# A two-layer graph kernel: attention in pairs of key blocks, and another order of work in the last block

## The chip, the cores and the metric

The kernel runs on one core of one Trainium2 chip. The metric is device time in microseconds (us) for one launch, and the number compared is the median over runs. A profiled execution is one run with the hardware profiler on. Its span is the time from the first to the last instruction.

Engines: PE is TensorE's matmul row, PEld its weight loads, DVE VectorE, ACT ScalarE, POOL GpSimd, SP SyncE, which here issues DMAs. L436 is line 436 of the kernel before.

## The reference, cut to what matters

There are 32 samples of 512 nodes with 512 features, all in fp32, and one 512 x 512 adjacency matrix for all samples. Layer 0 is a graph layer, layer 1 masked attention with 8 heads of 64. Each has a residual and a layernorm.

```
x = layernorm(x + deg * (x @ Wi.T + b) + adj @ (x @ Wj.T))     # layer 0
q, k, v = split_heads(x @ Wq.T + bq), ...                      # layer 1
scores = einsum('bhqd,bhkd->bhqk', q, k) / 8
scores = where(adj == 0, -inf, scores)
attn   = softmax(scores)
x = layernorm(x + (attn @ v) @ Wo.T + bo)
```

## The kernel before, in words

**Products.** Every 512 x 512 by 512 x 512 product (layer 0's two, q, k, v and the output projection) is done with seven half-size products in place of eight. Each is a *piece* (`piece`, L411 on): products 1 to 7, of kind l0, v, q, k or pj (projection). A piece is four matmuls with 256 columns (eight records in the profile, as an fp32 matmul leaves two); an l0 piece has twice as many, as it takes two weights. Its sums and differences of inputs come from `combos` on POOL (L405), its weights from DRAM through a ring of seven SBUF tiles that SP fills in order (`prefetch`, L286). It writes into one of two PSUM banks, "a" and "b" (`mm_tile`, one buffer each). The products fall into groups (X: 1, 2; Y: 6, 7, 4; Z: 5, 3), and those of a group add up in the same bank, so that each piece is read out by DVE or ACT before the next piece in its bank may write. Kinds are alternated between the two banks. DVE adds l0 and pj pieces to the rows (L454), v to v (L465), q and k with their bias (L481) or without (L474); ACT copies product 1 (L443) and writes product 2 of v (L463), q and k (L479).

**Attention.** A block of work is one sample's attention: 8 steps, `divmod(step, 4)` giving a group g of four heads and a block kc of 128 keys. A step does the following:
- `scores` twice: two heads at a time, two matmuls on 64 rows each into a PSUM tile "sc" of two banks. There are two such tiles. ACT takes the exponential in place (L494), DVE multiplies by the mask into an SBUF tile "e" (L495; four such buffers).
- `values` of the step before: eight matmuls of 32 columns each into two "ov" tiles (L512).
- at the last block of keys of a group, `sums` (denominators, L522, into an sc tile), `drain` by ACT (L527), and then `rest`: four reciprocals (`invert`, L531), two `scale` (L547) and `tell` (L535) on DVE.
- `presum`: e tiles of a group are added up, the first two on POOL (L501), the others on DVE (L503).

[...]

**Order.** Engines work through their queues in the order in which the program issues instructions; nothing reorders it (`manual_schedule`). The order is written by hand. While sample b = n - 1 has its attention, the pieces of layer 0, v, q, k of sample n and the projection of sample n - 2 fill the steps. `phase_b`, `phase_c` and `phase_a` list them with entries of no cost (`z`) between: statistics (`stats`: bn_stats and bn_aggr on DVE, then L300 to L302 on POOL), `apply` on ACT (L305), the rows' way through DRAM into transposed form (`h_store` on ACT's queue, `h_load` on SP's, `h_turn` on DVE, L382), `l0_gather` (L334, adjacency by rows, copied out by ACT, followed by `split`: a cast on ACT and a subtraction on POOL, L204), `l0_turn` (L348 on DVE, L349 on POOL), `base` (L354, DVE). `by_steps` deals the list out to the eight steps by the cost PC, TR or GA of each entry. For a middle block this gives:

```
0  l0_2  combos  pj1  l0_6  pj2
1  combos  l0_7  add_bo0  pj6  l0_4  stats(n,0)  pj7
2  apply(n,0)  h_store0  l0_5  h_load0  add_bo1  pj4  l0_3  stats(n,1)  h_turn0  pj5
3  apply(n,1)  h_store1  v1  pj3  h_load1  stats(m,0)  v2  stats(m,1)  q1  k1  apply(m,0)  h_turn1  q2
4  apply(m,1)  store  combos  k2  q5  v5  q3  v3
5  load_x  q6  v6  q7  v7  q4  v4  (with load_xa, ahead)
6  gather0  k5  turn0  gather1  k3  turn1  base0  combos  gather2  k6
7  turn2  base1  gather3  k7  turn3  combos  l0_1  k4
```

Here n is the sample in layer 0 and m = n - 2; k pieces of steps 6 and 7 use the bank that gathers do not use. Behind each piece or gather the main loop issues one presum that is due, and entries of `rest`.

**The end.** The last sample's attention has only the projection of the sample before it to fill its steps (`last_steps`), its own projection (`last_part`, L735 and L736, in four row blocks) and the last rows' layernorm (`last_rows`).

Of the kernel before, what the change touches and what calls it, by code (L numbers as in the profile page):

```python
# [17 lines left out]
P = 128  # L18
# [7 lines left out]
def gnn_attention_kernel(  # L26
# [53 lines left out]
    def work(shape, name, bufs, dtype=FT):  # L80
        return pools.work.tile(shape, dtype, name=name, bufs=bufs)
# [10 lines left out]
    def sc_tile():  # L92
        return psum.tile([P, 2, N], FT, name="sc", bufs=2)
# [189 lines left out]
    def prefetch():  # L283
        while len(TILES) < min(len(KEYS), ring.used + RING) and KEYS[len(TILES)] in WS:
            t = ring_tile()
            nc.sync.dma_start(t, WS[KEYS[len(TILES)]])  # L286
            TILES.append(t)
# [193 lines left out]
                    nc.vector.scalar_tensor_tensor(d[:, c], pm[:, c, :], bc, p1[:, c, :], op0=OP.add, op1=OP.add)  # L481


    E, ES, PV, RL = {}, {}, {}, {}

    def scores(b, hp, kc):
        ps = sc_tile()
        for s in range(2):
            r = slice(s * HD, (s + 1) * HD)
            nc.tensor.matmul(ps[:, s, :], KT[b, hp // 2][r, hp % 2, kc * P:(kc + 1) * P],  # L490
                             QT[b, hp // 2][r, hp % 2, :], start=True, stop=True)
        e = E[hp % 2, kc] = work([P, 2, N], "e", 4)

        nc.scalar.activation(ps, ps, AF.Exp, scale=QSCALE)  # L494
        nc.vector.tensor_tensor(e, ps, edge[:, kc:kc + 1, :].to_broadcast([P, 2, N]), op=OP.mult)  # L495

    def presum(i, kc):
# [7 lines left out]
    def values(b, g, kc):  # L505

        if kc == 0:
            PV[g] = [ov_tile(), ov_tile()]
        for r in range(2):
            for h in range(4):  # L510
                c0 = (4 * g + h) * HD + 32 * r
                nc.tensor.matmul(PV[g][r][32 * h:32 * h + 32, :], V[b][:, kc, c0:c0 + 32], E[h // 2, kc][:, h % 2, :],  # L512
                                 start=(kc == 0), stop=(kc == NC - 1))
# [12 lines left out]
        j = 2 * (b * 2 + g)  # L526
        nc.scalar.activation(RL[g][1], RL[g][0], AF.Identity, accum_out=told[:, j:j + 1])  # L527

    def invert(g, part, src=1):
        c = slice(part * P, (part + 1) * P)  # L530
        nc.vector.reciprocal(RL[g][1][:, c], RL[g][src][:, c])  # L531

    def tell(b, g):
        j = 2 * (b * 2 + g) + 1
        nc.vector.reduce_sum(told[:, j:j + 1], RL.pop(g)[1], axis=AX.X)  # L535

    def tell_all(b, g):

        pl, rl = RL.pop(g)
        j = 2 * (b * 2 + g)  # L540
        nc.gpsimd.memset(told[:, j + 1:j + 2], 0.0)
        nc.vector.tensor_tensor_reduce(pl, pl, rl, 1.0, 0.0, OP.add, OP.add, told[:, j:j + 1])

    def scale(b, g, r, c=slice(0, N)):
        if (b, g) not in OT:
# [14 lines left out]
    def z(f, *a):  # L560
        return (0.0, f, *a)

    def pc(kind, b, i, bank):
        return (2 * PC if kind == "l0" else PC, piece, kind, b, i, bank)
# [1 line left out]
    ORDER = (1, 2, 6, 7, 4, 5, 3)  # L566

    LATE = (5, 3, 6, 7, 4)
    ALONE = ((1, "a"), (6, "b"), (2, "a"), (7, "b"), (5, "a"), (4, "b"), (3, "a"))

    def banks(n):

# [2 lines left out]
    def phase_a(n):  # L575

        A, K = banks(n)
        if n == B:
            return [pc("k", n - 1, i, bank) for i, bank in ((6, K), (5, A), (7, K), (3, A), (4, K))]
        xq, aq = lambda j, m: quarter(XD[n], j, m), lambda j, m: quarter(AX_T[n], j, m)  # L580
        g = [(GA, l0_gather, n, dc, A) for dc in range(DC)]
        k = [pc("k", n - 1, i, K) for i in LATE]
        res = []
        for i in range(DC):
            res += g[i:i + 1] + k[i:i + 1] + [z(l0_turn, n, i)]
            if i in (1, 2):
                res += [z(base, n, i - 1)]
            if i == 1:
                res += [z(combos, TX, n, xq, (1,)), z(combos, TA, n, aq, (1,))]
        return res + [z(combos, TX, n, xq, (2,)), z(combos, TA, n, aq, (2,)),  # L590
                      z(combos, TX, n, xq, (3, 4)), z(combos, TA, n, aq, (3, 4)),
                      pc("l0", n, 1, A), k[4]]
# [27 lines left out]
    def project(m, i):  # L620

        res = [pc("pj", m, i, banks(m)[1])]
        if i == 1:
            res = [z(combos, TO, m, ot_quarter(m), (1,))] + res
        if i == 2:
            res = [FLUSH] + res + [z(combos, TO, m, ot_quarter(m), (2, 3, 4))]
        return res

    def phase_b(n):

        m = n - 2
        if m < 0:
            res = []
            side = [z(add_bo, 0, i) for i in range(2)]
            A, K = banks(n)
            for i, bank in ((2, A), (6, K), (5, A), (7, K), (4, K), (3, A)):
                res.append(pc("l0", n, i, bank))
                if i == 4:
                    res += [z(stats, n, 0)]
                if i in (2, 6):  # L640
                    res += [z(combine, "wo", nc.vector, int(i == 6))]
                res += side[:1]
                side = side[1:]
            return res + [z(apply, n, 0), z(stats, n, 1), (TR, l0_norm, n, 0), (TR, l0_norm, n, 1)]
        A = banks(n)[0]
        l0 = {i: pc("l0", n, i, A) for i in ORDER}
        return [l0[2], *project(m, 1), l0[6], *project(m, 2), l0[7], z(add_bo, n - 1, 0), *project(m, 6), l0[4], z(stats, n, 0),
                *project(m, 7), z(apply, n, 0), z(h_store, n, 0), l0[5], z(h_load, n, 0), z(add_bo, n - 1, 1), *project(m, 4),
                l0[3], z(stats, n, 1), z(h_turn, n, 0), *project(m, 5)]

    def phase_c(n):

# [53 lines left out]
    def last_steps():  # L706

        m = B - 2
        p = {i: pc("pj", m, i, bank) for i, bank in ALONE}
        c = [z(combos, TO, m, ot_quarter(m), (1, 2)), z(combos, TO, m, ot_quarter(m), (3, 4))]  # L710
        own = [(4 * GA, last_part, c, 0) for c in range(2)]
        return [[z(last_load), FLUSH, c[0], p[1], c[1]], [p[2], p[6]], [p[5], p[7], z(add_bo, B - 1, 0), z(add_bo, B - 1, 1)],
                [p[3], p[4], z(stats, m, 0), z(stats, m, 1)], [z(apply, m, 0), z(apply, m, 1), z(store, m)], [own[0]], [own[1]], []]

    def run(f):
        f[1](*f[2:])
# [8 lines left out]
    def last_part(c, half=None, ic=None):  # L725
        if c == 0:
            if half == 0:
                ACC[0], ACC[1] = mm_tile("a"), mm_tile("b")
            else:
                t = sc_tile()  # L730
                ACC[2], ACC[3] = t[:, 0, :], t[:, 1, :]
        for ic in (range(2 * half, 2 * half + 2) if ic is None else (ic,)):
            if c == 0:

                nc.tensor.matmul(ACC[ic], ident, XT[B - 1][:, ic, :], start=True, stop=False)  # L735
            nc.tensor.matmul(ACC[ic], OT[B - 1, c // 2][:, c % 2, ic * P:(ic + 1) * P], W["wo"][c // 2][:, c % 2, :],  # L736
                             start=False, stop=(c == 3))
# [32 lines left out]
    for f in PERIODS[0]:  # L770
        run(f)
        if f[1] is combine:
            prefetch()
    for n in range(1, B + 1):
        b = n - 1
        extra = []
        for step in range(STEPS):
            g, kc = divmod(step, NC)
            scores(b, 2 * g, kc)
            scores(b, 2 * g + 1, kc)  # L780
            pb, pg, pk = (b, *divmod(step - 1, NC)) if step > 0 else (b - 1, 1, NC - 1)
            if pb >= 0:
                values(pb, pg, pk)
                if pk == NC - 1:
                    sums(pg, *(((1, 3), 3) if pb == B - 1 else ()))
                    drain(pb, pg)
                    extra = rest(pb, pg)
            late = [(presum, i, kc) for i in range(2) if kc > 0]
            if b == B - 1 and kc > 2 - g:

                late = []
            for f in PERIODS[n][step]:
                if f is FLUSH:
                    some = len(extra)
                else:
                    run(f)

                    some = 0 if f[0] == 0.0 else len(extra) if step == 0 else max(1, round(f[0] / PC))
                if some:
                    for g in late[:1] + extra[:some]:  # L800
                        g[0](*g[1:])
                    late, extra = late[1:], extra[some:]
            for g in late + extra:
                g[0](*g[1:])
            extra = []
    sums(1, (1, 2), 3)
    values(B - 1, 1, 3)
    sums(1, (3,), 3)
    for c in range(2):
        last_part(c, 1)  # L810
    for ic in range(NC):
        c = slice(ic * P, (ic + 1) * P)
        invert(1, ic, 0)
        scale(B - 1, 1, 0, c)
        scale(B - 1, 1, 1, c)
        last_part(2, ic=ic)
        last_part(3, ic=ic)
        if ic > 0:
            last_rows(ic - 1)
    tell_all(B - 1, 1)  # L820
    last_rows(NC - 1)
    flags()
    fast.close()
# [139 lines left out]
```

## Time and profile before

| what | value |
|---|---|
| median of 10 runs | 3694.5 us (3692.47 to 3696.34) |
| profiled execution: its time | 3693.48 us |
| its span | 3691.7 us |
| PE, PEld busy | 3661.8, 2510.9 us |
| DVE, POOL, ACT busy | 2393.1, 1940.8, 1028.5 us |
| mean granted TensorE clock | 0.999 |
| DMA queue 1's share of the 16 engines | 49.4% |
| exponentials (L494), masks (L495) | 512 each, 1007 and 1217 ns |
| presums on DVE (L503), on POOL (L501) | 250 of 1217 ns, 128 of 2360 ns |

A matmul's end in the profile is modelled and neighbours overlap, so lengths of matmul work are read from start to start. "Idle before, releaser" tells which event ended an engine's idle time. Instructions that follow one another on an engine are merged in a timeline; the number behind the x counts them. In a timeline the first column is the start in us from the span's start, the second the length in us.

### The profile page before, as it was taken

The numbers are of one execution on the slowest core, as the hardware profiler recorded it, in microseconds if no ns is written. First come the engines' busy times: TensorE is split into PE (matmuls) and PEld (weight loads), VectorE is DVE, ScalarE is ACT, GpSimd is POOL, SyncE is SP. The second block draws the span as 40 slices with busy tenths as digits, with TensorE's granted clock in tenths as the row PEclk, the third lists the DMA queues.
The fourth block names the chain that finished last, engine by engine and source line by source line (L and its number), as shares of the span: only waits on it lengthen the run. The fifth ranks groups of instructions, "written<-read, shape, count | busy, mean of one in ns | idle before, by whom it ended". The sixth has DMA issues, their size and how long they took to land.

```text
span 3691.7 us, 49640 instructions
## 1 busy us (share of the span) xinstructions
PE 3661.8 (99%) x18470; PEld 2510.9 (68%) x18470; DVE 2393.1 (65%) x3134; ACT 1028.5 (28%) x1483; POOL 1940.8 (53%) x1985
## 2 busy tenths in 40 slices
PE   9999999999999999999999999999999999999997
PEld 6766667676667666767676767676767676767663
DVE  4666666666666666666666666666666666666665
ACT  2232232222322223222223222222222322222322
POOL 3565545556445555455554555644555545555443
PEclk9999999999999999999999999999999999999999
DMA  8445455445555445564455555455544555445541
GB/s 256 140 120 143 138 155 160 136 133 137 149 159 150 130 134 147 151 166 122 138 140 152 160 146 127 133 151 157 155 125 136 144 156 162 130 134 139 149 137 47
DMA packets 797173, 530.02 MB, mean 144 GB/s; under 512 B 530432, under 2 KB 611840, under 8 KB 796928
## 3 DMA queue, kind: packets, MB, share of 16 engines
q1 hardware_dynamic: 780384, 494.78, 49.4%
q10 hardware_dynamic: 16320, 31.46, 2.3%
q8 instruction: 151, 2.47, 0.3%
q14 instruction: 94, 0.77, 0.1%
q0 software_dynamic: 224, 0.53, 0.0%
HBM read 453.25 MB, written 73.40 MB: 143 GB/s over the span
## 4 chain that ended last, share of the span: by engine, by line
PE 98%; DVE 1%; POOL 0%; ACT 0%; issue 0%; DMA 0%; SPq 0%; ACTq 0%; DVEq 0%; POOLq 0%
PE mma L436 31%; PE mmb L436 31%; PE sc L490 13%; PE ov L512 13%; PE mmb L334 4%; PE mma L334 3%; PE sc L522 2%; PE mmb L611 0%; PE mma L611 0%; DVE rl L531 0%; DVE e L495 0%; PE sc L736 0%; DVE st L298 0%; POOL es L501 0%; DMA big<-in_adj_dram 0%
## 5 line engine op out<-in xcount | busy, mean ns | idle before, releaser
L494 ACT ACTIVATE sc<-sc 128x1024 f32<-128x1024 f32 x512 | 493.0, 1007 | 1554.8 <-PE sc L490 1548.8
L495 DVE TENSOR_TENSOR e<-sc,edge 128x1024 f32<-128x1024 f32 x512 | 602.2, 1217 | 212.1 <-ACT sc L494 179.7
L436 PE MATMUL mmb<-ring,big 128*128 128x256 f32 x3144 | 731.7, 381 | 0.0
L436 PE MATMUL mma<-ring,big 128*128 128x256 f32 x3112 | 724.4, 381 | 1.5 <-DVE xh L454 0.8
L436 PEld LDWEIGHTS mmb<-ring,big 128*128 128x128 f32 x3144 | 591.9, 190 | 131.6 <-issue 27.7
L436 PEld LDWEIGHTS mma<-ring,big 128*128 128x128 f32 x3112 | 585.8, 190 | 132.4 <-issue 26.5
L490 PE MATMUL sc<-q,k 64*128 64x512 f32 x2048 | 509.0, 615 | 0.0
L405 POOL TENSOR_TENSOR big<-big 128x512 f32<-128x512 f32 x376 | 492.3, 1338 | 28.4 <-ACT big L363 12.5
L512 PE MATMUL ov<-e,v 128*32 128x512 f32 x4096 | 492.5, 598 | 4.9 <-DVE oT L547 4.9
L501 POOL TENSOR_TENSOR es<-e 128x1024 f32<-128x1024 f32 x128 | 300.6, 2360 | 355.1 <-DVE e L495 355.1
L436 PE MATMUL mma<-big,ring 128*128 128x256 f32 x1808 | 430.3, 381 | 0.0
L436 PE MATMUL mmb<-big,ring 128*128 128x256 f32 x1776 | 422.8, 381 | 1.0 <-DVE v L465 1.0
L300 POOL TENSOR_SCALAR mv<-mv 128x1 f32<-128x1 f32 x256 | 50.1, 196 | 674.0 <-DVE mv L299 661.7
L436 PEld LDWEIGHTS mma<-big,ring 128*128 128x128 f32 x1808 | 340.5, 190 | 73.1 <-issue 26.0
L436 PEld LDWEIGHTS mmb<-big,ring 128*128 128x128 f32 x1776 | 334.3, 190 | 73.5 <-issue 26.0
L512 PEld LDWEIGHTS ov<-e,v 128*32 128x32 f32 x4096 | 106.9, 109 | 352.2 <-issue 320.8
L204 POOL TENSOR_TENSOR xlo<-xh,xhi 128x512 fp32r<-128x512 f32 x128 | 162.9, 1285 | 338.8 <-ACT xhi L203 338.7
L490 PEld LDWEIGHTS sc<-q,k 64*128 64x128 f32 x2048 | 176.0, 186 | 207.4 <-issue 205.1
L349 POOL TENSOR_TENSOR big<-big,deg_r 128x512 f32<-128x512 f32 x124 | 173.5, 1399 | 263.5 <-DVE big L348 263.5
L503 DVE TENSOR_TENSOR es<-es,e 128x1024 f32<-128x1024 f32 x250 | 304.1, 1217 | 0.0
L454 DVE TENSOR_TENSOR xh<-xh,mma 128x512 f32<-128x512 f32 x186 | 126.7, 681 | 263.5 <-PE mma L436 263.5
L454 DVE TENSOR_TENSOR xh<-xh,mmb 128x512 f32<-128x512 f32 x186 | 126.7, 681 | 259.3 <-PE mmb L436 259.3
(161 smaller groups left out, 3662.4 us busy)
## 6 DMA issues: line engine op xcount, KB each, us to landing
ring<-wo SPq DMA_DIRECT2D x217, 256.0 KB, 2.8
ring<-wq SPq DMA_DIRECT2D x160, 256.0 KB, 3.9
ring<-wv SPq DMA_DIRECT2D x160, 256.0 KB, 3.4
ring<-wk SPq DMA_DIRECT2D x160, 256.0 KB, 3.2
ring<-wi SPq DMA_DIRECT2D x155, 256.0 KB, 2.6
ring<-wj SPq DMA_DIRECT2D x155, 256.0 KB, 2.6
xh<-in_x_dram SPq DMA_DIRECT2D x32, 1024.0 KB, 5.4
xa<-in_x_dram SPq DMA_DIRECT2D x124, 256.0 KB, 3.9
```

Source lines behind the costliest of these rows:

```text
L204: nc.gpsimd.tensor_sub(lo, xs, hi.bitcast(FT))
L334: nc.tensor.matmul(pm, parts[w][:, jc, :], adjR[:, jc, :], start=(w == 0 and jc == 0), stop=(w == 1 and jc == NC - 1))
L349: nc.gpsimd.tensor_tensor(XD[b][:, dc, :], XD[b][:, dc, :], deg_r, op=OP.mult)
L405: nc.gpsimd.tensor_tensor(dst, p, q, op=OP.subtract)
L436: nc.tensor.matmul(pm[:, c * Q:(c + 1) * Q], lhs, rhs, start=first, stop=(kc == 1 and n == len(terms) - 1), skip_group_check=True)
L454: nc.vector.tensor_tensor(d, d, pm, op=OP.add)
L490: nc.tensor.matmul(ps[:, s, :], KT[b, hp // 2][r, hp % 2, kc * P:(kc + 1) * P], QT[b, hp // 2][r, hp % 2, :], start=True, stop=True)
L494: nc.scalar.activation(ps, ps, AF.Exp, scale=QSCALE)
L495: nc.vector.tensor_tensor(e, ps, edge[:, kc:kc + 1, :].to_broadcast([P, 2, N]), op=OP.mult)
L501: nc.gpsimd.tensor_add(ES[i], E[i, 0], E[i, 1])
L503: nc.vector.tensor_add(ES[i], ES[i], E[i, kc])
L512: nc.tensor.matmul(PV[g][r][32 * h:32 * h + 32, :], V[b][:, kc, c0:c0 + 32], E[h // 2, kc][:, h % 2, :], start=(kc == 0), stop=(kc == NC - 1))
```

## The change

It has two parts.

**Attention in four steps of two blocks of keys.** For all samples but the last, the main loop goes two steps at a time. It issues the scores of the first block of keys, the values of both blocks that are due, the masks of the first block, and at a group's end sums, drain and rest; then the scores of the second block, and then the pieces of both steps. The mask leaves `scores` and becomes an operation of its own. The masks of the second block, `tell` and the presums (four for kc = 2, 3, two for kc = 0, 1) are issued one by one behind pieces; at a group's end the reciprocals and scales are issued before the pieces, otherwise the first of these masks is. In the list, `apply(n,0)` and `h_store0` come ahead of pj7, `h_load0` ahead of l0_5, `h_turn0` ahead of l0_3; nothing is issued between l0_3 and `stats(n,1)`.

**The end.** Of the last sample's five remaining k pieces, 7 and 4 move into its first attention step; the projection before it takes the usual order of pieces, with 3 and 4 one step each behind; statistics, apply and store of that sample move behind it. The final denominators are drained by ACT and inverted in SBUF; the last two row blocks get an sc tile each and their first two parts are issued between those of the first two.

```diff
     def scores(b, hp, kc):
...
+        SC[hp] = ps
+
+        nc.scalar.activation(ps, ps, AF.Exp, scale=QSCALE)
+
+    def mask(hp, kc):
+        ps = SC.pop(hp)
         e = E[hp % 2, kc] = work([P, 2, N], "e", 4)
-
-        nc.scalar.activation(ps, ps, AF.Exp, scale=QSCALE)
         nc.vector.tensor_tensor(e, ps, edge[:, kc:kc + 1, :].to_broadcast([P, 2, N]), op=OP.mult)
...
-        return [l0[2], *project(m, 1), l0[6], *project(m, 2), l0[7], z(add_bo, n - 1, 0), *project(m, 6), l0[4], z(stats, n, 0),
-                *project(m, 7), z(apply, n, 0), z(h_store, n, 0), l0[5], z(h_load, n, 0), z(add_bo, n - 1, 1), *project(m, 4),
-                l0[3], z(stats, n, 1), z(h_turn, n, 0), *project(m, 5)]
+                z(apply, n, 0), z(h_store, n, 0), *project(m, 7), z(h_load, n, 0), l0[5], z(add_bo, n - 1, 1), *project(m, 4),
+                z(h_turn, n, 0), l0[3], z(stats, n, 1), *project(m, 5)]
...
+        k = [pc("k", B - 1, i, K) for i in (7, 4)]
+        return [[z(last_load), k[0], FLUSH, c[0], p[1], c[1], k[1]], [p[2], p[6]], [p[5], p[7], z(add_bo, B - 1, 0), z(add_bo, B - 1, 1)],
+                [p[3]], [p[4]], [own[0], z(stats, m, 0), z(stats, m, 1)], [own[1], z(apply, m, 0), z(apply, m, 1), z(store, m)], []]
...
+        alone = b == B - 1
+        size = 1 if alone else 2
+        for step in range(0, STEPS, size):
             g, kc = divmod(step, NC)
+            extra = []
+            for i in range(2):
+                scores(b, 2 * g + i, kc)
+            for f in due:
+                values(*f)
+            for i in range(2):
+                mask(2 * g + i, kc)
+            if due and due[-1][2] == NC - 1:
+                pb, pg = due[-1][:2]
+                sums(pg, *(((1, 3), 3) if pb == B - 1 else ()))
+                drain(pb, pg)
+                extra = rest(pb, pg)
+            due = [(b, g, kc + i) for i in range(size)]
+            late = [(presum, i, c) for _, _, c in due if c > 0 for i in range(2)]
+            if alone:
...
+            else:
+                for i in range(2):
+                    scores(b, 2 * g + i, kc + 1)
+                late = [(mask, 2 * g + i, kc + 1) for i in range(2)] + extra[-1:] + late
+
+                for f in extra[:-1] if extra else late[:1]:
+                    f[0](*f[1:])
+                late, extra = late[0 if extra else 1:], []
+            for f in [f for todo in PERIODS[n][step:step + size] for f in todo]:
...
+                    if f[1] is piece and f[2] == "l0" and f[4] == 3:
+
+                        some = 0
                 if some:
                     for g in late[:1] + extra[:some]:
                         g[0](*g[1:])
...
     sums(1, (3,), 3)
-    for c in range(2):
-        last_part(c, 1)
+    drain(B - 1, 1)
     for ic in range(NC):
         c = slice(ic * P, (ic + 1) * P)
-        invert(1, ic, 0)
+        invert(1, ic)
         scale(B - 1, 1, 0, c)
         scale(B - 1, 1, 1, c)
+        if ic < 2:
+            last_part(0, 1, ic + 2)
+            last_part(1, 1, ic + 2)
         last_part(2, ic=ic)
         last_part(3, ic=ic)
```

More of the change, by code (lines that the diff above doesn't have):

```diff
@@ L481, in piece @@
                     nc.vector.scalar_tensor_tensor(d[:, c], pm[:, c, :], bc, p1[:, c, :], op0=OP.add, op1=OP.add)
-    E, ES, PV, RL = {}, {}, {}, {}
+    SC, E, ES, PV, RL = {}, {}, {}, {}, {}
     def scores(b, hp, kc):
@@ L527, in drain, with invert @@
         nc.scalar.activation(RL[g][1], RL[g][0], AF.Identity, accum_out=told[:, j:j + 1])
-    def invert(g, part, src=1):
+    def invert(g, part):
         c = slice(part * P, (part + 1) * P)
-        nc.vector.reciprocal(RL[g][1][:, c], RL[g][src][:, c])
+        nc.vector.reciprocal(RL[g][1][:, c], RL[g][1][:, c])
     def tell(b, g):
@@ L535, in tell @@
         nc.vector.reduce_sum(told[:, j:j + 1], RL.pop(g)[1], axis=AX.X)
[L537 to L542, printed above, removed]
     def scale(b, g, r, c=slice(0, N)):
@@ L568, in gnn_attention_kernel @@
     LATE = (5, 3, 6, 7, 4)
-    ALONE = ((1, "a"), (6, "b"), (2, "a"), (7, "b"), (5, "a"), (4, "b"), (3, "a"))
     def banks(n):
@@ L578, in phase_a @@
         if n == B:
-            return [pc("k", n - 1, i, bank) for i, bank in ((6, K), (5, A), (7, K), (3, A), (4, K))]
+            return [pc("k", n - 1, i, bank) for i, bank in ((5, A), (6, K), (3, A))]
         xq, aq = lambda j, m: quarter(XD[n], j, m), lambda j, m: quarter(AX_T[n], j, m)
@@ L708, in last_steps @@
         m = B - 2
-        p = {i: pc("pj", m, i, bank) for i, bank in ALONE}
+        A, K = banks(B)
+        p = {i: pc("pj", m, i, K if i in (6, 7, 4) else A) for i in ORDER}
         c = [z(combos, TO, m, ot_quarter(m), (1, 2)), z(combos, TO, m, ot_quarter(m), (3, 4))]
         own = [(4 * GA, last_part, c, 0) for c in range(2)]
-        return [[z(last_load), FLUSH, c[0], p[1], c[1]], [p[2], p[6]], [p[5], p[7], z(add_bo, B - 1, 0), z(add_bo, B - 1, 1)],
-                [p[3], p[4], z(stats, m, 0), z(stats, m, 1)], [z(apply, m, 0), z(apply, m, 1), z(store, m)], [own[0]], [own[1]], []]
+        k = [pc("k", B - 1, i, K) for i in (7, 4)]
+        return [[z(last_load), k[0], FLUSH, c[0], p[1], c[1], k[1]], [p[2], p[6]], [p[5], p[7], z(add_bo, B - 1, 0), z(add_bo, B - 1, 1)],
+                [p[3]], [p[4]], [own[0], z(stats, m, 0), z(stats, m, 1)], [own[1], z(apply, m, 0), z(apply, m, 1), z(store, m)], []]
     def run(f):
@@ L729, in last_part @@
             else:
-                t = sc_tile()
-                ACC[2], ACC[3] = t[:, 0, :], t[:, 1, :]
+                ACC[ic] = sc_tile()[:, 0, :]
         for ic in (range(2 * half, 2 * half + 2) if ic is None else (ic,)):
@@ L773, in gnn_attention_kernel @@
             prefetch()
+    due = []
     for n in range(1, B + 1):
         b = n - 1
-        extra = []
-        for step in range(STEPS):
+        alone = b == B - 1
+        size = 1 if alone else 2
+        for step in range(0, STEPS, size):
             g, kc = divmod(step, NC)
[L779 to L792, printed above, removed]
+            extra = []
[13 more added lines that the diff above has]
+            if alone:
+                if kc > 2 - g:
+                    late = []
+            else:
[6 more added lines that the diff above has]
+            for f in [f for todo in PERIODS[n][step:step + size] for f in todo]:
                 if f is FLUSH:
@@ L795, in gnn_attention_kernel @@
                 else:
+                    if f[1] is l0_norm:
+                        for g in late:
+                            g[0](*g[1:])
+                        late = []
                     run(f)
-                    some = 0 if f[0] == 0.0 else len(extra) if step == 0 else max(1, round(f[0] / PC))
+                    some = 0 if f[0] == 0.0 else len(extra) if step == 0 and alone else max(1, round(f[0] / PC))
+                    if f[1] is piece and f[2] == "l0" and f[4] == 3:
+                        some = 0
                 if some:
@@ L804, in gnn_attention_kernel @@
                 g[0](*g[1:])
-            extra = []
     sums(1, (1, 2), 3)
@@ L819, in gnn_attention_kernel @@
             last_rows(ic - 1)
-    tell_all(B - 1, 1)
+    tell(B - 1, 1)
     last_rows(NC - 1)
```

## The prediction

> **What bounds the kernel now.** I read the busy shares and the chain first, then the matmuls of one block in order of time, then the whole trace for holes in TensorE's row, then one stretch with VectorE and GpSimd beside it.
>
> ```profile
> PE 3661.8 (99%) x18470; PEld 2510.9 (68%) x18470; DVE 2393.1 (65%) x3134; ACT 1028.5 (28%) x1483; POOL 1940.8 (53%) x1985
> ...
> PE 98%; DVE 1%; POOL 0%; ACT 0%; issue 0%; DMA 0%; SPq 0%; ACTq 0%; DVEq 0%; POOLq 0%
> ```
>
> TensorE sets the time. So only two things count: the time that its own instructions take, and new holes between them. The timeline of TensorE over one step (start, us, what) shows what a change of shape costs:
>
> ```profile
> 1841.55 1.99 PE L490 MATMUL sc<-q,k 64*128 64x512 f32 x8
> 1843.47 1.93 PE L512 MATMUL ov<-e,v 128*32 128x512 f32 x16
> 1845.33 1.99 PE L436 MATMUL mma<-ring,big 128*128 128x256 f32 x8
> 1847.16 1.89 PE L436 MATMUL mmb<-ring,oT 128*128 128x256 f32 x8
> 1848.88 1.89 PE L436 MATMUL mma<-ring,big 128*128 128x256 f32 x8
> ...
> 1859.54 1.04 PE L522 MATMUL sc<-es,ones 128*32 128x512 f32 x8
> ```
>
> A piece takes 1.73 us from start to start, but 1.83 when it comes first after values. From the starts of the single matmuls (steady spacing 216 ns in pieces, 429 ns in scores, values and sums) the changes cost: into scores 93 + 104 = 197 ns, into values 97 + 25 = 122 ns, into pieces 113 + 104 = 217 ns, from values into sums nothing. Between 160 and 3570 us no other hole over 0.3 us exists. The steady kernel has no stall to remove, only these changes.
>
> The last block differs, and shows how a hole arises:
>
> ```profile
> 3588.03 1.89 PE L436 MATMUL mmb<-ring,big 128*128 128x256 f32 x8
> 3590.90 1.99 PE L436 MATMUL mmb<-big,ring 128*128 128x256 f32 x8 [0.98 <-DVE v L465]
> ...
> 3646.80 1.93 PE L512 MATMUL ov<-e,v 128*32 128x512 f32 x16 [3.09 <-DVE oT L547]
> ```
>
> A piece waits until VectorE has read the piece before it out of the same bank. VectorE was late because two presums (1.2 us each) stood in its queue.
>
> The stretch of steps 6 and 7 is the one to watch (TensorE, VectorE and GpSimd of one timeline):
>
> ```profile
> 1892.97 1.89 PE L436 MATMUL mma<-big,ring 128*128 128x256 f32 x8
> ...
> 1896.54 1.89 PE L436 MATMUL mma<-big,ring 128*128 128x256 f32 x8
> ...
> 1896.60 3.42 DVE L354 SCALAR_TENSOR_TENSOR xh<-b_r,deg_c,xh 128x512 f32<-128x512 f32 x2 [0.21 <-POOL xlo L204]
> ...
> 1897.88 3.28 POOL L405 TENSOR_TENSOR big<-big 128x512 f32<-128x512 f32 x2
> 1898.36 1.99 PE L490 MATMUL sc<-q,k 64*128 64x512 f32 x8
> 1899.94 0.68 DVE L474 TENSOR_TENSOR k<-mma,k 128x512 f32<-128x512 f32 x1
> ...
> 1904.09 1.89 PE L436 MATMUL mma<-big,ring 128*128 128x256 f32 x8
> ```
>
> k6 ends at about 1898.3 and is read out only at 1899.94, behind base (3.42 us). Nobody waits: scores and values of step 7 fill 3.8 us, and k7 starts at 1904.09.
>
> [...] 122 to 217 ns per change, and none from values to sums, which are tiled alike. [...] 124 of 128 base operations lie on a GpSimd one and the median is 1.75 us, against 0.71 for those that meet it late or not; presums beside add_bo took 1.76 and 1.70 us instead of 1.21.
>
> **The change, part by part.** I call the new pairs 0-1, 2-3, 4-5 and 6-7, and count t from a pair's first scores.
>
> *Fewer changes of shape.* Two old steps have scores, values and pieces twice: 2 x (197 + 122 + 217) = 1072 ns. A pair has scores, values (both blocks), scores, pieces. Values to scores is not in the steady trace; one sums-to-scores change shows the 113 ns of its class, so I take 97 + 104 = 201 (bounds 0[...], and 217). New sum 197 + 122 + 201 + 217 = 737. Gain 0.335 us per pair (0.32 to 0.54), 31 blocks x 4 pairs: **-41.5 us** (-40 to -67).
>
> *Do the second scores wait for their tiles?* First masks need the e buffers that the first values release, at t = 1.92 + 1.93 + 0.06 = 3.9. Two masks take 2.35, so the second tile is free at 6.3. TensorE ends both values at 5.49 and needs the first tile (free 5.1) at 5.6, the second at 6.55. Where sums lie between, sums take the first tile, scores need the second at 6.46. Slack 0.15 to 0.25 us: nothing lost while VectorE and ScalarE are on time. Pieces start at 7.5 (8.4 with sums). In 2-3 they are not quite on time: apply and h_store of half 0 now stand in ScalarE's queue ahead of the exponentials, and wait for the statistics (GpSimd needs 1.2 us for each block of rows), so that the exponentials start at 3.3 to 3.6 instead of 1.2: 0.1 to 0.5 us, I take 0.3.
>
> *6-7: the pause is gone, four presums stand before k6's read-out.* TensorE: gather0 7.5-9.55, k5 to 11.3, gather1 13.1, k3 14.85, gather2 16.7, k6 18.4, gather3 20.26, then k7. VectorE in order: k5 read-out from 11.45 (0.80), presum 1.13, turn 0.62, presum 1.13 (now 15.13), k3 0.80 (15.93), presum 1.13, turn 0.62 (17.7), base 3.35 (21.05), presum 1.13 (22.2), k6 0.69: 22.9. k7 waits 22.9 - 20.26 = 2.7 us. Before, two of these presums came after k7's start. If base met no GpSimd work (2 x 0.71) it would be 0.7; if, as the order of the queues suggests, GpSimd's turn product and xlo also catch the third and fourth presum, these add up to 2.0: 4.7. I take 3.6. 30 blocks have gathers: **+108 us** (20 to 141).
>
> *2-3: v2 waits for v1's copy.* l0[3] ends at 16.2; VectorE reads it out to 17.0, statistics to 18.7, GpSimd's chain ends 20.4 to 20.6 (before: 4.4 us after l0[3]), apply to 21.3, the h_store issue up to 0.37, only then ScalarE copies v1 (0.6): 21.9 to 22.4. v2 could start at 21.4. Before, scores and values (3.8 us) lay between. 0.5 to 1.0, I take 0.7; with the 0.3 above 1.0 x 30 = **+30 us** (18 to 45).
>
> *4-5: reciprocals and scales in one run.* Sums end 6.35, drain ends 7.3, four reciprocals 3.4, two scales 1.3: 12.0. Then a mask (13.2), q5's read-out (14.0). q3 could start at 13.65: 0.4 x 30 = **+12 us** (0 to 20). In 0-1 the first piece is an l0 one of 3.5 us and ends at 11.9, so VectorE is back in time: nothing. If that cover were a short piece, the same 0.4 would appear there.
>
> *Moves with no path cost.* h_load 0 passes l0[5] on SP: it waits for h_store, about 3.4 us, with ring prefetches behind it, covered by seven ring tiles (12 us of pieces); uncovered it would cost up to 3.4 us a block. h_turn 0 ahead of l0[3]: 1.25 us of VectorE, which is idle then. h_turn 1 is late in 4-5 only if its load comes after t = 3.9; I get 2.6, as apply is earlier by the 1.9 us of exponentials. Presums on GpSimd end before the masks that reuse their inputs (26.6 against 32).
>
> *The end.* The last 135 us hold some 9.7 us of holes, of 0.4 to 3.1 us. Two k pieces now fill the step after the first denominators (about -1.4) and statistics no longer precede the masks (-2.0). p4 in step 4 delays the reciprocals by its own 1.9 + 0.65, so that hole stays. The final denominators go through ScalarE (+0.7), the row blocks' own tiles free VectorE from the 1.5 us wait on ScalarE. Sum **-4** (-8 to +2). The first pair of block 0 has no values to cover its masks: **+2** (0 to 3).
>
> Against the profiled execution's 3693.5 us (span 3691.7 and 1.8 around it): 3693.5 - 41.5 + 108 + 30 + 12 - 4 + 2 = 3800.0. The median of the runs is 1.0 higher: **3801 us**, +2.9%.
>
> **Rivals.** *Forecast, bank waits outweigh the changes saved:* for it, VectorE's queue in 6-7 counted instruction by instruction and the 3590.90 line; against it, the size hangs on how GpSimd's operations fall. Range 3735 to 3850. Chance 0.66.
> *Faster, the bank waits don't hold TensorE:* one mechanism: read-outs keep ahead of the same bank's next piece, as they do throughout the steady trace. It decides where the waits of a block sum to less than 4 x 0.335 = 1.34 us. Then 3693.5 - 41.5 - 4 + 2 + 30 x 0.3 = 3659, median 3660. For it: nothing waits today. Against it: the 3.8 us pause that hid the late read-out is what is removed. 0.17.
> *Same:* base and presums meet no GpSimd work: 0.7 in 6-7, 0.5 in 2-3, none in 4-5: -43.5 + 36 = 3686 to 3700. 0.05.
> *Slower elsewhere, the score tiles:* if VectorE begins the first masks late by one mask (1.2 us), the second scores lose about 0.95 in each pair: -43.5 + 118 = 3768, and up to 3830 with bank waits on top. For it: the slack of 0.15 to 0.25. Against: VectorE is idle at t = 1 to 3.9. 0.12.
>
> **Numbers.** Within 0.2% (7 us) counts as same, about what a measurement of this kernel can tell. Faster 0.17, same 0.05, slower 0.66 + 0.12 = 0.78. From 3688 to 3850 leaves out the faster case and a few in a hundred above: it holds 0.8.
>
> **What would show it.** Right: k7's matmuls wait for "DVE k L474" in 6-7 (30 times, 2.7 to 4.7 us), a v piece waits for "ACT p L443" (0.5 to 1.0), a q piece for "DVE q L481" (0.4), and the changes of shape fall by a third. TensorE's busy share falls by 3 points. Wrong: no such waits (faster), or the waits stand at scores for "DVE e" (score tiles). A base that lasts 1.4 us in place of 3.4 would take 2 us off each block.

## The result, and the profile after

The change makes the kernel **slower by 10.3%**: 4075.6 us (median of 8 runs, 4071.4 to 4076.4) against 3693.7 (median of 28 runs), a ratio of 1.1032 [1.1022, 1.1042]. The prediction had the direction and most of the places, and missed the size by 275 us: it gave 3801, at most 3850. Two items make up most of the miss: the hole before v2 was nearly six times as long as forecast (100 us), and a clock at half rate behind the holes was not in the sum at all (98.5 us). The profiled execution has a span of 4073.6 us against 3691.7, so there are 381.9 us to find.

The page first: the busy shares, and the chain of work that ended last, by engine.

```profile
PE 3768.7 (93%) x18470; PEld 2593.9 (64%) x18470; DVE 2428.3 (60%) x3133; ACT 1047.3 (26%) x1485; POOL 2081.0 (51%) x1984
...
PE 73%; DVE 12%; POOL 8%; issue 4%; ACT 3%; ACTq 0%; DMA 0%; DVEq 0%; SPq 0%; POOLq 0%
```

Two things are to be seen. TensorE has fallen from 99% to 93%, and a quarter of the chain now runs through other engines. But TensorE is also busy for 107 us longer (3768.7 against 3661.8) with the same 18470 records: the work itself has become slower. The mean granted clock says how: 0.964 in place of 0.999.

Next the list of waits (engine, tile and line, then what it waited for; us in total, times, longest in us). These rows are TensorE's larger ones:

```profile
PEld sc L490 <- DVE e L499: 177.3, 191, 2.3
...
PE mma L436 <- DVE k L474: 67.4, 15, 4.5
PE mmb L436 <- DVE k L474: 65.4, 15, 4.5
PE mmb L436 <- ACT p L443: 57.9, 15, 3.9
PE mma L436 <- ACT p L443: 57.9, 15, 3.9
...
PE sc L490 <- DVE e L499: 23.4, 33, 1.5
```

The first row is of weight loads; at 2057.21 us, for one, they show 0.85 us of waiting where the matmuls beside them show none. What reaches the matmuls is in the other rows. They are the waits that the prediction named: a piece that waits for VectorE's read-out of k6 (30 times, up to 4.5 us), one that waits for ScalarE's copy of v1 (30 times, 3.9 us where 0.5 to 1.0 was forecast), and second scores that wait for a mask.

To split the 382 us I took every matmul's start, subtracted the steady spacing of its kind (216 ns in pieces, 429 ns in scores, values and sums), and sorted what is left by size and place. In us, over the whole span:

| | holes over 0.3 us | loss at half clock | shorter waits and changes of shape |
|---|---|---|---|
| before | 16.8 | 0 | 140.8 |
| after | 320.2 | 98.5 | 121.4 |
| difference | +303 | +98.5 | -19 |

The holes of after are k7 in 6-7 (29 of 4.67 and a first one of 2.64, 138 us), v2 in 2-3 (30 of 4.03, 121 us), the second scores of 2-3 (30 of 0.86, 26 us), 51 short ones of 0.37 to 0.39 (19 us, q3 in 4-5 among them), and 16 us at both ends of the kernel, as before. How much falls under half clock depends somewhat on the spacing that is taken as steady. The last column holds the saving: 335 ns a pair, 41.4 us, of which new waits of under 0.3 us give 22 back.

**The hole at v2.** This is the timeline of 2-3 in the block around 2040 us, cut to the instructions concerned (start, us, engine and line; at the end in brackets the idle time before it and what ended it):

```profile
2035.97 2.35 DVE L507 TENSOR_TENSOR es<-es,e 128x1024 f32<-128x1024 f32 x2
2036.05 1.19 POOL L300 TENSOR_SCALAR mv<-mv 128x1 f32<-128x1 f32 x1
2036.31 1.89 PE L436 MATMUL mmb<-ring,oT 128*128 128x256 f32 x8
2037.32 1.41 POOL L301 TENSOR_TENSOR mv<-mv,mhalf 128x1 f32<-128x1 f32 x1
2038.84 1.30 POOL L302 TENSOR_SCALAR mv<-mv 128x1 f32<-128x1 f32 x1
2038.85 1.25 DVE L507 TENSOR_TENSOR es<-es,e 128x1024 f32<-128x1024 f32 x1
...
2040.17 0.81 ACT L305 ACTIVATE xh<-xh,mv 128x512 f32<-128x512 f32 x1 [3.36 <-POOL mv L302]
...
2041.43 0.59 ACT L443 COPY p<-mma 128x512 f32<-128x512 f32 x1 [0.44 <-ACT xh L305]
2042.07 2.86 PE L436 MATMUL mma<-ring,big 128*128 128x256 f32 x8 [3.86 <-ACT p L443]
```

Read it from the bottom. v2 waits 3.86 us for the bank of v1; ScalarE copies v1 only at 2041.43, since it first does `apply`, which waits for L302. GpSimd's three statistics operations are on a single column and take 0.19, 0.55 and 0.27 us elsewhere in this trace (their medians); here they take 1.19, 1.41 and 1.30, 3.9 us together. VectorE is meanwhile in presums (L507): two in a row, those issued behind pj5 and v1, and a third, issued behind pj3, that meets L302 since the first two have made it late (in e3, below, L302 is over before that presum starts).

**The hole at k7.** The timeline of 6-7, fifty us on:

```profile
2094.59 1.55 DVE L507 TENSOR_TENSOR es<-es,e 128x1024 f32<-128x1024 f32 x1
2095.37 1.89 PE L436 MATMUL mma<-big,ring 128*128 128x256 f32 x8
...
2097.30 3.44 DVE L354 SCALAR_TENSOR_TENSOR xh<-b_r,deg_c,xh 128x512 f32<-128x512 f32 x2 [0.54 <-POOL xlo L204]
...
2100.66 2.28 DVE L507 TENSOR_TENSOR es<-es,e 128x1024 f32<-128x1024 f32 x1
2102.86 0.68 DVE L474 TENSOR_TENSOR k<-mma,k 128x512 f32<-128x512 f32 x1
2103.60 3.78 PE L436 MATMUL mma<-big,ring 128*128 128x256 f32 x8 [4.50 <-DVE k L474]
```

k6 (2095.37) is over by 2097.3 and is read out at 2102.86, behind both halves of base and a presum, as the prediction listed them. What it did not list is the last line's duration: k7 takes 3.78 us, where k6 took 1.89.

**Half clock.** The view of stretches gives the granted clock (PEclk, the third number from the end) in the 10 us around that hole, as a mean: 6.83 of the 10 us ran at half rate.

```profile
2100.00:2110.00 10.00, 6.40 (x20) 5.33 (x21) 7.78 (x8) 0.00 (x0) 4.74 (x4) 0.66 0.10 26
```

In the whole trace there are 60 stretches at half clock besides the end, one behind each of the 60 holes before k7 and v2, 37 of 3.41 us and 23 of 6.83. Counted from the start of the first of them, the 60 begin and end on whole multiples of 3.4133 us, to 0.01 us. A hole's length alone does not decide: the first hole before k7, of 2.64 us, brought a stretch, while one of 3.05 us at 4028 us brought none. What else decides was not shown.

### The profile page after: what moved, and what is told of

It reads as the page before. It is cut to its first block, busy times and chain, and to the rows that moved or that the text cites. A ratio compares the mean times of both kernels' runs of the same rounds, so it can differ in the third digit from the quotient of the medians.

```text
span 4073.6 us, 49647 instructions
## 1 busy us (share of the span) xinstructions
PE 3768.7 (93%) x18470; PEld 2593.9 (64%) x18470; DVE 2428.3 (60%) x3133; ACT 1047.3 (26%) x1485; POOL 2081.0 (51%) x1984
## 4 chain that ended last, share of the span: by engine, by line
PE 73%; DVE 12%; POOL 8%; issue 4%; ACT 3%; ACTq 0%; DMA 0%; DVEq 0%; SPq 0%; POOLq 0%
PE mma L436 24%; PE mmb L436 24%; PE sc L490 11%; PE ov L516 10%; DVE rl L535 3%; POOL xlo L204 2%; DVE e L499 2%; DVE es L507 2%; POOL big L349 2%; PE sc L526 1%; DVE xh L354 1%; POOL mv L301 1%; PE mmb L334 1%; POOL mv L302 1%; DVE oT L544 1%
## 5 line engine op out<-in xcount | busy, mean ns | idle before, releaser
L436 PE MATMUL mma<-big,ring 128*128 128x256 f32 x1808 | 472.0, 408 | 71.2 <-DVE k L474 67.4
L436 PE MATMUL mmb<-big,ring 128*128 128x256 f32 x1776 | 459.1, 405 | 68.7 <-DVE k L474 65.4
L204 POOL TENSOR_TENSOR xlo<-xh,xhi 128x512 fp32r<-128x512 f32 x128 | 190.6, 1499 | 570.5 <-ACT xhi L203 570.5
L516 PE MATMUL ov<-e,v 128*32 128x512 f32 x4096 | 466.8, 595 | 2.9 <-DVE oT L544 2.9
L436 PEld LDWEIGHTS mma<-big,ring 128*128 128x128 f32 x1808 | 367.0, 206 | 154.2 <-DVE k L474 73.8
L305 ACT ACTIVATE xh<-xh,mv 128x512 f32<-128x512 f32 x252 | 197.6, 809 | 947.4 <-POOL mv L302 947.4
L300 POOL TENSOR_SCALAR mv<-mv 128x1 f32<-128x1 f32 x256 | 79.8, 312 | 521.9 <-DVE mv L299 509.4
L507 DVE TENSOR_TENSOR es<-es,e 128x1024 f32<-128x1024 f32 x250 | 344.2, 1388 | 0.0
L349 POOL TENSOR_TENSOR big<-big,deg_r 128x512 f32<-128x512 f32 x124 | 198.4, 1600 | 223.7 <-DVE big L348 214.9
L451 POOL TENSOR_TENSOR xh<-xh,p 128x512 f32<-128x512 f32 x186 | 231.2, 1271 | 145.2 <-ACT p L443 145.2
```

What stands on the lines that cost most here:

```text
L204: nc.gpsimd.tensor_sub(lo, xs, hi.bitcast(FT))
L305: nc.scalar.activation(y, y, AF.Identity, bias=mv[:, 4:5], scale=mv[:, 3:4])
L349: nc.gpsimd.tensor_tensor(XD[b][:, dc, :], XD[b][:, dc, :], deg_r, op=OP.mult)
L436: nc.tensor.matmul(pm[:, c * Q:(c + 1) * Q], lhs, rhs, start=first, stop=(kc == 1 and n == len(terms) - 1), skip_group_check=True)
L451: nc.gpsimd.tensor_tensor(d, d, p1, op=OP.add)
L507: nc.vector.tensor_add(ES[i], ES[i], E[i, kc])
```

## The experiments

Theory: in each block two bank waits cost 8.6 us, v2's through GpSimd's statistics being held up by VectorE's presums, k7's through presums and base ahead of k6's read-out, and each sets off a half-clock stretch as well. Rivals: v2 waits for the order on ScalarE alone; k7 waits for base alone, or for the presums alone; the end is to blame. No kernel here leaves any of the work out. Each of e2, e3, e4, e6, e7 and e9 was run once. "Holes" and "half clock" are those of the table above, in us.

### e1: the end alone

The loop goes back to single steps, with the old order in `phase_b`; the new end stays.

```diff
-        size = 1 if alone else 2
+        size = 1
```

Expected:

> Only the second part of the change: the end as in the changed kernel, the main loop in single steps as before. The prediction's own term says -4 us (-8 to +2), so 3689.5 (ratio 0.998 to 1.0005). If part of the 382 us came from the end, this would be slower than before.

Measured: 3687.25 us (16 runs), ratio 0.9983 [0.9975, 0.9990], or -6.2 us. The end is a small gain, and all of the loss comes with the first part of the change.

### e2: v1's copy ahead of apply

```diff
-            res = [z(apply, n, 1), z(h_store, n, 1), v[1], *project(m, 3), ...
+            res = [v[1], z(apply, n, 1), z(h_store, n, 1), *project(m, 3), ...
```

Expected:

> The changed kernel with v1 issued ahead of apply and h_store of half 1, so that ScalarE's copy of v1 no longer stands behind apply. The hole of 3.9 us before v2 (30 times, 116 us) must go, and with it the half clock that follows (some 45 to 65 us): about 3900. The rows' way through DRAM starts no earlier, so a new wait of 0.3 to 1.5 us at the first masks of steps 4 and 5 is possible (up to 45 us back). If the hole before v2 stayed, v1's copy wasn't its cause.

Measured: 3959.7 us, 116 less than after. The hole at v2 is gone. Yet the run fell 60 us short of the forecast. ScalarE's copy of v2 (L463) now stands behind `apply`, and k1, the next piece in its bank, waits 0.63 us for it, 30 times. And something else was late (timeline of e2, the step after):

```profile
2119.42 1.25 DVE L382 STREAM_TRANSPOSE big<-xa 128x1024 f32<-128x1024 f32 x1 [6.91 <-DMA xa<-hd]
...
2121.83 1.06 PE L526 MATMUL sc<-es,ones 128*32 128x512 f32 x8 [1.25 <-DVE e L499]
```

With `apply` and `h_store` later, the load that follows them is later too, and `h_turn`, which reads it, keeps VectorE's queue at a stand for 6.9 us with the next masks behind it. 24 holes of 0.5 to 1.4 us at the sums cost 22 us. The half clock fell by some 40 us, where 45 to 65 was expected.

### e3 and e7: no presum, or one, beside the statistics

After leaves the place behind l0[3] free of presums. e3 leaves those behind pj5 and v1 free too, e7 only that behind v1.

```diff
-                    if f[1] is piece and f[2] == "l0" and f[4] == 3:
+                    if f[1] is piece and n > 1 and (f[2], f[4]) in (("l0", 3), ("pj", 5), ("v", 1)):     # e3
+                    if f[1] is piece and n > 1 and (f[2], f[4]) in (("l0", 3), ("v", 1)):                # e7
```

Expected:

> The changed kernel, but no presum is issued behind pj5 and v1, so that VectorE's two-input additions do not run beside GpSimd's small chain of the statistics. ScalarE's order is unchanged. [...] the chain takes 2.4 us again in place of 5.3, the hole before v2 falls from 3.9 to the 0.5 to 1.0 of the prediction, and no half clock follows there: 4075 - 30 x (3.1 + 1.5 to 2.2) = 3916 to 3937. Rival, ScalarE's queue order alone explains the hole: it stays at 3.9 and the time near 4075.

> The changed kernel with one of the two presums between l0_3 and v2 held back (the one behind v1), the other left. With none there the hole before v2 was 1.15 us, with two 4.0. [...] GpSimd's chain is held by one presum, so 2.2 to 3.0. Half clock: if it needs a hole above 3.3 us (the kernel before had one of 3.3 without it), none follows here, and the time is 4075 - 30 x (1.0 to 1.8) - 35 to 50 = 3970 to 4010; if any hole over 2 us brings it, 4020 to 4045.

Measured: e3 3949.9 us, 13 above its range, as a hole of 1.15 us stayed and the half clock fell by 40 us only; e7 3975.4, inside its range. The order on ScalarE is that of after, and the hole at v2 still shrinks with the number of presums issued behind pj5 and v1: 4.03 us with two, 2.13 with one, 1.15 with none. The timeline of e3 at the same three operations:

```profile
2097.88 0.19 POOL L300 TENSOR_SCALAR mv<-mv 128x1 f32<-128x1 f32 x1
2098.16 0.55 POOL L301 TENSOR_TENSOR mv<-mv,mhalf 128x1 f32<-128x1 f32 x1
2098.81 0.27 POOL L302 TENSOR_SCALAR mv<-mv 128x1 f32<-128x1 f32 x1
```

and that of e7, where one presum is left:

```profile
2113.24 1.22 DVE L507 TENSOR_TENSOR es<-es,e 128x1024 f32<-128x1024 f32 x1
2113.31 1.19 POOL L300 TENSOR_SCALAR mv<-mv 128x1 f32<-128x1 f32 x1
2114.59 0.55 POOL L301 TENSOR_TENSOR mv<-mv,mhalf 128x1 f32<-128x1 f32 x1
```

With none beside it L300 takes 0.19 us; with one it starts 0.07 us behind the presum and ends with it, while L301, free of it, takes its 0.55. So it is in after: the 30 L300 that start beside a presum take 1.19 to 1.20 us and end 0.05 us behind it. A GpSimd operation of 0.19 us waited out a whole presum of 1.22 each time. So the rival "order alone" accounts for 1.15 of the 4.03 us, and the hold-up for the rest. Both are needed: in e2 L300 still takes over 0.9 us in 30 blocks, as in after, and v2 does not wait.

### e4 and e6: base or the presums away from k6's read-out

e4 issues base two pieces later, behind k6 and k7; e6 holds back the presums that would be issued behind gather1, gather2 and k3, so that they come later.

```diff
-            res += g[i:i + 1] + k[i:i + 1] + [z(l0_turn, n, i)]
-            if i in (1, 2):
-                res += [z(base, n, i - 1)]
+            res += g[i:i + 1] + k[i:i + 1]
+            if i in (2, 3):
+                res += [z(base, n, i - 2)]
+            res += [z(l0_turn, n, i)]
```

```diff
+                    if n > 1 and step == 6 and (f[1] is l0_gather and f[3] in (1, 2) or f[1] is piece and (f[2], f[4]) == ("k", 3)):
+                        some = 0
```

Expected:

> The changed kernel with base of each half issued behind k6 and k7 in place of ahead of k6, so that VectorE reads k6 out before base. The hole of 4.6 us before k7 (138 us) should go, as by the count k6 is then read out at 19.5 and k7 could start at 20.3. [...] the half-clock stretch behind it goes too (another 45 to 65): about 3880. If the half clock has a cause of its own, 3937. If the presums alone hold k6 up, a hole of about 1 stays.

> The changed kernel with base where it was, ahead of k6, and the presums that followed gather1, k3 and gather2 issued behind k6 and later. If base alone (3.4 us) makes the hole before k7, it stays above 3 us and the time above 4000. If presums and base together do, as counted, k6 is read out at 20.6 and k7 could start at 20.3: a hole of 0.2 to 0.8, no half clock there, about 3885 to 3905.

Measured: e4 3879.7 us, e6 3930.4. In e4 the k7 hole is gone, and holes and half clock fall by 137 and 55 us, together 192 of the 196 us that it gained. In e6 the same hole shrinks from 4.6 to 0.59 us, though base stands where it did (timeline of e6; the first column is the start):

```profile
2148.29 3.44 DVE L354 SCALAR_TENSOR_TENSOR xh<-b_r,deg_c,xh 128x512 f32<-128x512 f32 x2 [0.21 <-POOL xlo L204]
2151.65 0.68 DVE L474 TENSOR_TENSOR k<-mmb,k 128x512 f32<-128x512 f32 x1
2152.38 1.99 PE L436 MATMUL mmb<-big,ring 128*128 128x256 f32 x8 [0.42 <-DVE k L474]
...
2158.66 1.99 PE L436 MATMUL mmb<-big,ring 128*128 128x256 f32 x8 [0.83 <-DVE k L474]
```

So neither base nor the presums alone make this hole; either is borne, both together are not. e6 misses its forecast by 25 us: its presums, moved behind k6, delay k7's own read-out (last line), and 30 new holes of 1.0 us at k4 cost 30.

### e9: only the exponentials of 2-3 first

`apply(n,0)` and `h_store0` go behind pj7 again, and where a step's list begins with them they are issued ahead of the second scores.

```diff
-                z(apply, n, 0), z(h_store, n, 0), *project(m, 7), z(h_load, n, 0), l0[5], ...
+                *project(m, 7), z(apply, n, 0), z(h_store, n, 0), z(h_load, n, 0), l0[5], ...
...
+                while PERIODS[n][step] and PERIODS[n][step][0][1] in (apply, h_store):
+                    run(PERIODS[n][step].pop(0))
```

Expected:

> The changed kernel with only apply and h_store of half 0 moved behind the first exponentials of steps 2 and 3. The prediction gave these exponentials 0.3 us a block, the profile after shows scores of steps 2 and 3 late by 0.86 - 0.11 and a further 0.27 inside them: 1.0 x 30. So 4045, and the holes before v2 and k7 as they were. If the score tiles of steps 2 and 3 are late for another reason, 4075.

Measured: 4074.0 us, 1.6 less than after and inside the spread of after's runs, where a gain of some 30 was expected. The wait itself went as expected: the holes at the second scores of 2-3 fall from 0.86 to 0.11 us. But the mean clock fell to 0.951, and the half-clock loss rose from 98.5 to 117.9 us, as 56 of its 59 half-clock stretches besides the end last 6.83 us, where 37 of after's 60 lasted 3.41. The view of stretches of e9 shows the six us behind a hole, with TensorE busy throughout at a mean clock of 0.66:

```profile
2102.00:2108.00 6.00, 6.00 (x19) 4.94 (x20) 3.95 (x5) 0.00 (x0) 2.70 (x2) 0.66 0.16 44
```

From one block's first gather to the next, after and e9 take the same 126.3 us on the mean of the steady blocks, 37.00 times 3.413. So this wait cost nothing as long as the two big holes were there: taken away, its time returned, as half clock for the most part.

### e5 and e8: the causes removed together

e5 joins e4's place of base, e2's order, e3's free places (and one behind k2) and e9's edit. e8 also moves `h_turn(n,1)` behind q2, where it comes to be issued behind the first masks.

```diff
-                   q[1], k[1], z(apply, m, 0), z(h_turn, n, 1), q[2], z(apply, m, 1), z(store, m),
+                   q[1], k[1], z(apply, m, 0), q[2], z(h_turn, n, 1), z(apply, m, 1), z(store, m),
...
-                while PERIODS[n][step] and PERIODS[n][step][0][1] in (apply, h_store):
+                while PERIODS[n][step] and PERIODS[n][step][0][1] in (apply, h_store, h_turn):
```

Expected:

> The changed kernel with every wait that was found taken out by order alone: base behind k6 and k7; no presum behind pj5, v1 and k2; v1 ahead of apply and h_store of half 1; apply (and h_store of half 0, again behind pj7) issued between the first and the second scores, behind the first exponentials. If the changes of shape are the gain of the pairs (41.5 us) and the waits are all their loss: before's 3693.5 - 6.2 for the end - 41.5 + 3 to 12 for the score tiles' slack = 3649 to 3658, ratio 0.988 to 0.9905. If pairs are slower in themselves (two-block values, score tiles), it stays above 3687.

> The mended kernel with h_turn of half 1 issued behind the first masks of steps 4 and 5 instead of ahead of them, as there it waits for its load and the masks, and with them the sums, wait behind it (13 holes of 0.4 to 1.6 us, 10 us in the profiled run, and some smaller ones at the second scores). Those go: 3664 to 3670, ratio 0.9915 to 0.9935, and the runs spread less than 8 us. If the holes come from the masks themselves (e buffers, score tiles), the time stays at 3673 to 3682.

Measured: e5 3678.6 us (5 runs), ratio 0.9956 [0.9942, 0.9970]; its 13 holes at sums (9.8 us), behind an `h_turn` that waits for its load (2.75 us in the block at 2083 us), account for part of its miss of 21 us. **e8 3662.8 us** (5 runs, 3661.4 to 3663.6), ratio 0.9913 [0.9900, 0.9927]: faster than both kernels, 31 us under before and 1 under its range. Its holes are 16.7 us, as before's were, and the shorter losses 108.8 against 140.8: the saving of the pairs is what is left over. The 5 us to the upper end of e5's forecast stay unexplained. The page of e8, and its timeline of a pair that ends a group:

```profile
PE 3632.2 (99%) x18470; PEld 2524.6 (69%) x18470; DVE 2385.0 (65%) x3133; ACT 1028.3 (28%) x1485; POOL 2057.5 (56%) x1984
```

```profile
2071.74 1.99 PE L490 MATMUL sc<-q,k 64*128 64x512 f32 x8
2073.66 3.64 PE L516 MATMUL ov<-e,v 128*32 128x512 f32 x32
...
2077.11 1.04 PE L526 MATMUL sc<-es,ones 128*32 128x512 f32 x8
...
2078.09 2.02 PE L490 MATMUL sc<-q,k 64*128 64x512 f32 x8
2080.05 1.99 PE L436 MATMUL mma<-big,ring 128*128 128x256 f32 x8
```

No line has a wait: scores, both values, sums, scores, piece follow one another. The same 18470 matmuls take 29.6 us less of TensorE's time than before (3632.2 against 3661.8).

## Why the prediction was right or wrong

Its own terms, in us of the whole span, with what the traces measure:

| term | predicted | measured |
|---|---|---|
| fewer changes of shape | -41.5 | -41.4 |
| 6-7, k7 waits for k6's read-out | +108 | +138 |
| 2-3, v2 waits for v1's copy | +21 | +121 |
| 2-3, second scores late | +9 | +34 |
| 4-5, q3 | +12 | +11.6 |
| the end and the first pair | -2 | -1 |
| half clock | no term | +98.5 |
| waits under 0.4 us elsewhere | no term | +22 |
| sum | +106.5 | +382 |

- **Changes of shape: right.** Values to scores, which the trace of before did not show, costs 113 + 104 ns, where 97 + 104 was taken, and pieces behind scores cost 97 + 104, where 113 + 104 was taken. The two were exchanged, and a pair costs the 737 ns of the sum. e8 shows it as a gain.
- **6-7: right in mechanism, low in size.** 4.6 us against 3.6 taken, inside the bound of 4.7. The case behind that bound happened: the presums met GpSimd's work (1.55 and 2.28 us in the fence above, in place of 1.2) and base waited 0.54 us for xlo. The presums' 1.4 us and this wait are the 2.0 us of the bound. e4 and e6 both support the queue as it was counted.
- **2-3, v2: the step that failed.** The words "GpSimd's chain ends 20.4 to 20.6 (before: 4.4 us after l0[3])" took the chain's length from before, where no presum stood beside it. The prediction knew the hold-up between the two engines and used it for base and presums in 6-7, but not for the statistics in 2-3, where the presums behind pj5 and v1 now fall. The chain's last three operations take 3.9 us in place of 1.0, so `apply` and the copy come about 3 us later: 4.0 in place of 0.7, 100 us in 30 blocks. e3 and e7 show it.
- **2-3, second scores: too small.** 0.86 of hole and 0.27 within the scores, 1.1 in place of 0.3: `apply` and `h_store` kept the exponentials longer. e9 shows that they are the cause, and that the price was nothing while the big holes stood.
- **4-5: right.** 0.386 us, 30 times.
- **Half clock: no term at all.** The trace of before has a hole of 3.3 us at 3646.80 (its listed wait is 3.09) that brought no half clock, and I did not ask what a longer one does. The holes taken in 6-7, 3.6 with a bound of 4.7 us, are longer than that one, so the clock needed a term. It costs 1.4 us for a v2 hole (e4, which has hardly any others of that size: 43 us in 30) and 2.0 for a k7 hole (e3, 59 in 29).
- **The end: right in sign**, -6.2 against -4. The first pair's cost, unsplit from it in after, is then about 5 where 2 was taken.
- **The rivals.** *Same* and *faster* fell. Of *slower elsewhere* a form came true: exponentials, not VectorE, made score tiles late, in one pair of four. The range ended at 3850, and even all upper bounds together (-40 + 141 + 45 + 20 + 2 + 3) give only 3866, as no bound holds the half clock or the longer chain.

Open: why e9's block keeps 37.00 times 3.413 us. The stretches of after end on multiples of 3.4133 us too, so an earlier hole could bring a longer stretch; e7's block is 36.00 times 3.413 us and e4's 35.05, but those of e2, e3 and e6 are not whole (35.9, 35.8, 35.5), so that this is argued, not shown.

## What to carry to other kernels

When two stretches of a busy engine are put together, list for each PSUM bank what now stands in the queue of the engine that reads it out, and for each of these what it waits for in turn, down to the smallest operation: here columns of 128 numbers on GpSimd held TensorE. Price a hole twice, by its length and, where the trace shows half clock behind holes like it (here behind all 59 of 4.0 and 4.7 us), by that stretch; so a saving of 1.3 us a block became a loss of 12. And undo the causes together: single mends returned 100 to 196 us on the large waits and next to nothing on the small one, and only the set of them brought the gain.

## What the runs showed of the hardware

- **The hold-up works both ways, and on GpSimd's side by whole instructions.** Before showed base slowed beside GpSimd's work (0.71 to 1.75 us); here a GpSimd operation of 0.19 us, on 128 x 1 elements, took 1.19 beside a presum of 1.22 on VectorE. The measured form is a wait to the end of the other's instruction: in after the 30 operations of this kind (L300) ended 0.05 us behind their presum.
- **Half clock came behind long holes, but a hole's length alone does not decide.** In after, the holes of 4.0 and 4.7 us brought it every time (59 of 59). Shorter ones brought it or not: 2.64 us in after did; 3.3 in before, 3.05 in after and the 2.1 of e7 did not. (As e7's block is 36.00 times 3.413 us long, and the stretches of after begin on multiples of 3.413, its 30 holes may not be 30 independent samples.) A stretch of after, the end aside, lasts 3.41 us (37 of 60) or 6.83 (23).
- **A shorter schedule can gain nothing.** In its one run e9 removed 26 us of holes at the scores and 9 of shorter waits, and got 19 back as half clock and 13 as other holes under 0.5 us.
